# Weight loads of a two-part kernel on ScalarE's queue instead of SyncE's, and one preparation item a product later

## The chip, the cores and the metric

The kernel runs on one core of a Trainium2 chip. The metric is the time of one execution on the device in microseconds (us). Engines are called TensorE (PE in the profile; PEld is its weight load), VectorE (DVE), ScalarE (ACT), GpSimd (POOL) and SyncE (SP). A transfer (DMA) is issued by an engine in the order of that engine's instructions, goes into that engine's queue, and is carried out by 16 DMA engines that all queues share.

## The reference

The input `x` is 4 x 1024 x 1024 in float32. With `xn` the layer norm of `x`, the output is `x + s * g`:

```python
# s: an attention without softmax, over 4096 tokens of 1024 features
q, k, v = xn @ Wq.T + bq, xn @ Wk.T + bk, xn @ Wv.T + bv
kv = cumsum((elu(k) + 1) * v, axis=1)
s = ((elu(q) + 1) * kv * 64 ** -0.5) @ Wo.T + bo
# g: tokens are dispatched to 8 experts by the router's top 2, at most 256 places an expert;
# all experts have the same weights
h = gelu(buf @ w1.T + b1) @ w2.T + b2          # w1 4096 x 1024, w2 1024 x 4096
g = silu(sum over kept places of h * probability)
```

A token that no expert keeps has g = 0 there, and its output is `x`.

## The kernel before

Every product in float32 precision is made of three float32r matmuls: each operand is split into a high part (a cast by ScalarE, line 863) and a low part (VectorE's subtraction of the high part, line 866), and high x high, high x low and low x high are added up.

**The first part** (to about 453 us of the profiled execution) normalizes tokens, multiplies by Wk and Wv, makes the running sums, and routes the tokens. **The second part** has the 2048 chosen tokens, in two halves of 1024 (p = 0 and p = 1). For each half come five pairs of matrix products: four slices of the hidden layer (`hidden`, features x tokens, then `ffn_out`, tokens x outputs), and then `queries` with Wq and `result` with Wo. Each of these ten matrix products is done by a scheme of seven block products instead of eight, so there are 140 block products in a row, 14 for each pair, 48 matmuls each. They are called products 1 to 140 here; p = 1 begins with product 71.

The second part is written in steps, one for each product, step n beside product n. `on(n, phase, f)` puts a piece of work into a step, and the steps are emitted in an order by hand that every engine and SyncE's queue keep:

```python
PHASES = ("load", "pre", "cast0", "evac", "low0", "add", "cast1", "mid", "low1", "post", "raw")
for n in range(-4, n0 + 2):
    if 1 <= n <= n0:
        multiply(n)
    for phase in PHASES: ...        # the pieces of step n
```

What the next product needs is made in step n: the high parts of its two halves in `cast0` and `cast1`, the low parts in `low0` and `low1`. Each half has a buffer of its own out of three for a side (`Unit`), so a buffer is free when the product half that used it, three halves back, is done. `evac` adds up finished products, `add` and `post` make the sums of blocks that the scheme needs (line 1045, `sub`), and `raw`, the last phase, issues loads of weights.

There are two sorts of loads:

- **Raw weights** (tiles `raw`, five buffers of 128 x 4 x 512): quarters of a weight matrix, 1 MB a load, that ScalarE and VectorE turn into operands. `left_weights` (through `left_quarter`, line 834) loads those of w1 and Wq, `right_weights` (line 1184) those of w2. Four loads come in the four steps before the matrix product that uses them. A load waits until the tile's last reader is done.
- **Right operands that are stored ready** (tile `b`, line 1091, `fetched`): the tokens' operands (`xtd`, written on the way when the first slice of a half needs them, or by `xprep_items`) and those of Wo (`wod`, by `wprep_items`). They are loaded in phase `load` of the step before their product, in two halves of 1 MB.

Both sorts are issued by SyncE, in the order of the steps.

In the first half, three other pieces of work lie beside the products. `xprep_items` gathers the tokens of the second half and writes their operands, in steps 13 to 19 and 28 to 34; `wprep_items` does it for Wo, in four items of six stages that begin in steps 8, 20, 25 and 37 (load by GpSimd, then sums and subtractions of VectorE, casts of ScalarE, stores by GpSimd); and `queries` gathers the running sums. All their transfers go through GpSimd's queue (q0 in the profile). SyncE's queue is q1, ScalarE's q10.

Of the kernel before, what the change touches and what calls it, by code (L numbers as in the profile page):

```python
# [46 lines left out]
def tile_first_tokens(  # L47
# [17 lines left out]
    nc = tc.nc  # L65
# [107 lines left out]
    def split(dst, src):  # L173

        nc.scalar.copy(dst[0], src)  # L175
        nc.vector.tensor_tensor(dst[1], src, dst[0].bitcast(F32), ALU.subtract)  # L176
# [65 lines left out]
    def in_turn(ins):  # L242

        tc.keep_in_program_order(ins)
        return ins
# [477 lines left out]
    def wprep_items(w, buf):  # L723

        def item(a, k):
            v = {}

            def fetch():  # L730
                for j in range(2):
                    r = buf(f"wr_{a}_{k}_{j}")
                    for i in range(2):
                        v[i, j] = r[:, i * BT : (i + 1) * BT]
                        row = w[j, 2 * i + a].rearrange("p k f -> p (k f)")
                        in_turn(nc.gpsimd.dma_start(v[i, j], row[:, k * BT : (k + 1) * BT]))

            def out_of(i, src):
                o = buf(f"wo_{a}_{k}_{i}")
                oh = o.bitcast(F32R).rearrange("p (h t) -> h p t", h=2)  # L740
                split((oh[0], oh[1]), src)
                dst = wod.rearrange("(i p) (u h k t) -> i p u h k t", i=7, u=2, h=2, k=2)[i - 1]
                in_turn(
                    nc.gpsimd.dma_start(dst[:, a, :, k], o.rearrange("p (h t) -> p h t", h=2))  # L744
                )

            def sums():
                t = buf(f"wt_{a}_{k}")
                v["t1"], v["t2"] = t[:, :BT], t[:, BT:]
                nc.vector.tensor_tensor(v["t1"], v[0, 1], v[0, 0], ALU.subtract)  # L750
                nc.vector.tensor_tensor(v["t2"], v[1, 1], v["t1"], ALU.subtract)

            def out1():
                out_of(1, v[0, 0])
                out_of(2, v[1, 0])

            def out2():
                out_of(6, v["t2"])
                nc.vector.tensor_tensor(v[1, 0], v[1, 0], v["t2"], ALU.subtract)
                out_of(4, v[1, 0])  # L760

            def out3():
                out_of(3, v[1, 1])
                nc.vector.tensor_tensor(v[0, 1], v[1, 1], v[0, 1], ALU.subtract)
                out_of(7, v[0, 1])

            def out4():
                out_of(5, v["t1"])

            return fetch, sums, out1, out2, out3, out4  # L770

        return [item(a, k) for a in range(2) for k in range(2)]
# [56 lines left out]
        nc.vector.tensor_tensor(work[:, 2], work[:, 3], work[:, 2], ALU.subtract)  # L829
        nc.vector.tensor_tensor(ht, work[:, 2], work[:, 0], ALU.add)  # L830

    def left_quarter(dst, src, i, j):

        nc.sync.dma_start(
            dst.rearrange("p m (k f) -> p m k f", k=4),
            src[4 * i : 4 * i + 4, :, 4 * j : 4 * j + 4].rearrange("m p k f -> p m k f"),
        )
# [40 lines left out]
    raw = [early.tile([P, 4, BT], F32, name=f"raw_{i}") for i in range(2)]  # L878
# [138 lines left out]
    def on(n, phase, f):  # L1017
        hooks.setdefault((n, phase), []).append(f)
# [25 lines left out]
    def sub(dst, a, b):  # L1044
        nc.vector.tensor_tensor(dst, a, b, ALU.subtract)  # L1045

    def plus(dst, a, b):
        nc.vector.tensor_tensor(dst, a, b, ALU.add)  # L1048
# [17 lines left out]
    def built(n, side, src, halves, view):  # L1066

        units = plan_at(n)[side]
        plan_at(n)[side + "view"] = view
        if n == 1:  # L1070
            units.update(enumerate(begun[side]))
            return
        for u in range(2):

            def cast(u=u):
                x = Unit(side, 2 * n + u)
                x.cast(halves(src())[u])
                units[u] = x

            on(n - 1, f"cast{u}", cast)  # L1080
            on(n - 1, f"low{u}", lambda u=u: units[u].low())
# [66 lines left out]
    def left_weights(n0, src, order):  # L1148

        if order == ROWS:  # L1150
            tiles = ((0, 0), (1, 0), (1, 1), "t", (0, 1))
            loads = ((-4, (0, 0)), (-3, (1, 0)), (-2, (1, 1)), (-1, (0, 1)))
            if n0 % PASS == 0:

                loads = ((-10, (0, 0)), (-9, (1, 0)), (-8, (1, 1)), (-6, (0, 1)))
            on(n0, "add", lambda: sub(q["t"], q[0, 0], q[1, 0]))
            on(n0 + 1, "pre", lambda: plus(q[1, 0], q[1, 0], q[1, 1]))
            on(n0 + 1, "pre", lambda: sub(q[0, 0], q[1, 0], q[0, 0]))
        else:
            tiles = ((0, 0), (0, 1), (1, 0), (1, 1), "t")  # L1160
            loads = ((-4, (0, 0)), (-3, (0, 1)), (-2, (1, 0)), (-1, (1, 1)))
            on(n0 + 1, "add", lambda: sub(q["t"], q[0, 0], q[1, 0]))

            on(n0 + 1, "post", lambda: sub(q[0, 0], q[1, 1], q["t"]))
            on(n0 + 2, "add", lambda: plus(q[1, 0], q[1, 0], q[1, 1]))
        on(n0 + 3, "add", lambda: sub(q[0, 1], q[0, 1], q[0, 0]))
        q = dict(zip(tiles, raw))
        raw[:] = (q[k] for k in ((0, 0), "t", (1, 0), (1, 1), (0, 1)))
        for d, key in loads:

            if n0 or d > -3:
                on(max(n0 + d, -1), "raw", lambda key=key: left_quarter(q[key], src, *key))
        of = {1: (0, 0), 2: (0, 1), 3: (0, 1), 4: (1, 1), 5: (1, 0), 6: (0, 0), 7: "t"}
        for k, i in enumerate(order):
            built(n0 + 1 + k, "a", lambda i=i: q[of[i]], by_blocks, of_blocks)

    def right_weights(n0, src):

        q = dict(zip(((0, 0), (0, 1), (1, 1), "t", (1, 0)), raw))
        raw[:] = (q[k] for k in ("t", (0, 1), (0, 0), (1, 1), (1, 0)))  # L1180

        def load(key):
            i, j = key
            nc.sync.dma_start(
                q[i, j].rearrange("p (a k) f -> p a (k f)", a=2),
                src[j, 2 * i : 2 * i + 2].rearrange("a p k f -> p a (k f)"),
            )

        for d, key in ((-4, (0, 0)), (-3, (0, 1)), (-2, (1, 1)), (-1, (1, 0))):
            on(n0 + d, "raw", lambda key=key: load(key))  # L1190

        def t1():
            sub(q["t"], q[0, 1], q[0, 0])
            sub(q[0, 1], q[1, 1], q[0, 1])

        on(n0 - 1, "post", t1)
        on(n0, "post", lambda: sub(q[0, 0], q[1, 1], q["t"]))
        on(n0 + 5, "add", lambda: sub(q[1, 0], q[1, 0], q[0, 0]))
        for k, key in enumerate(((0, 0), (1, 0), (0, 0), "t", (0, 1), (1, 1), (1, 0))):
            built(n0 + 1 + k, "b", lambda key=key: q[key], by_chunks, all_chunks)  # L1200
# [38 lines left out]
    def features(n0, p, src, act, then=None, order=ROWS):  # L1239

        h = dict(hq)
        left_weights(n0, src, order)
        right_tokens(n0, p, order)
        if order == ROWS:
# [64 lines left out]
    def hidden(n0, p, s):  # L1309
        def act(dst, src, i, j):  # L1310
            for m in range(4):
                fc = s * DC + i * 4 + m
                nc.scalar.activation(dst[:, m], src[:, m], AF.Gelu, bias=b1[:, fc : fc + 1])  # L1313

        return features(
            n0, p, w1[s * DC : (s + 1) * DC], act, order=ROWS if s else FIRST
        )
# [206 lines left out]
    n0 = 0  # L1524
    for p in range(NP):
        y = dict(yq)
        if p == 0:
            for k, f in zip((8, 20, 25, 37), wprep_items(wo[0], small)):
                for d, stage in zip((0, 1, 1, 2, 3, 4), f):
                    on(n0 + k + d, "post" if d else "load", stage)  # L1530
        if p + 1 < NP:
            prep = xprep_items(p + 1, small)
            ats = ((0, 2, 2, 2, 2, 3, 3, 3, 4), (2, 4, 4, 5, 4, 5, 5, 6, 6))
            for j, (k, at) in enumerate((k, at) for k in (13, 28) for at in ats):
                for i, (d, f) in enumerate(zip(at, prep[j])):
                    on(n0 + k + d, "post" if i else "load", f)
        for s in range(NQ):
            h = hidden(n0, p, s)
            ffn_out(n0 + 7, h, s, y)
            n0 += 14  # L1540
        h = queries(n0, p)
        finals(n0, y, p)
        result(n0 + 7, h, y, p)
        n0 += 14
# [87 lines left out]
```

## Time and profile before

| | us |
|---|---|
| median of 3 runs | 2049.31 |
| lowest, highest | 2042.5, 2054.33 |
| the profiled execution's own time | 2028.41 |
| its span, first to last instruction | 2026.6 |
| products 1 to 140 | 453 to 2006 |

| transfers in the profile's list | issued by | count | KB each |
|---|---|---|---|
| b<-xtd, b<-wod | SyncE | 126, 28 | 1024 |
| raw<-in_w, raw<-in_wq | SyncE | 64, 8 | 1024 |
| xtd<-o, wod<-wo | GpSimd | 28, 28 | 512 |
| wr<-in_wo | GpSimd | 16 | 256 |
| kvs<-kr (first part) | ScalarE | 32 | 256 |

A line of a timeline gives the start in us, the duration (of merged instructions from the first start to the last end), engine, line of the program, operation and tiles, and in brackets the idle time before it and what ended that. A q behind an engine's name (SPq) marks its instruction sequencer: for a transfer it is the issue, not the transfer itself. Starts of products are taken from the trace: every 48th matmul of line 1121.

### The profile page before, as it was taken

Reading aid. Unit: us, or ns where it says so; the run is one execution under the profiler, and the core shown is the slowest. Engines: PE = TensorE matmul, PEld = TensorE weight load, DVE = VectorE, ACT = ScalarE, POOL = GpSimd, SP = SyncE. Lnnn points to the kernel's source line nnn. Section 1 sums busy time; section 2 is a strip of 40 time slices with the busy share of each in tenths; the row PEclk is TensorE's granted clock in tenths of the full one; section 3 lists DMA queues with packets and bytes.
Section 4 is the critical chain, followed back from the end, with each engine's and each line's share of the span. In section 5 each row is a group of like instructions: output and inputs, shape, how many; then the busy total and the mean of one; then the engine's idle time right before and its main releaser. Section 6 shows DMA issues by size and latency. Waiting matters only on the chain.

```text
span 2026.6 us, 22522 instructions
## 1 busy us (share of the span) xinstructions
PE 1973.7 (97%) x8872; PEld 1627.0 (80%) x8872; DVE 1509.2 (74%) x1422; ACT 747.8 (37%) x876; POOL 413.5 (20%) x403
## 2 busy tenths in 40 slices
PE   8999999999999999999899999999999999999995
PEld 7877878788888787887688888888888888888884
DVE  7868876488897896894497796596586586697794
ACT  3323332225534443542242452352342342342460
POOL 2001103550043124117203015500000000303014
PEclk9999999999999999999799999999999999999998
DMA  8768848638359559547515579814614614715567
GB/s 313 239 198 239 270 133 177 188 123 306 112 203 347 208 203 368 218 150 246 196 46 196 185 241 324 296 42 166 249 42 167 249 42 166 270 44 195 187 203 152
DMA packets 121011, 400.17 MB, mean 197 GB/s; under 512 B 13792, under 2 KB 38368, under 8 KB 99168
## 3 DMA queue, kind: packets, MB, share of 16 engines
q1 hardware_dynamic: 79360, 320.95, 45.7%
q0 software_dynamic: 23104, 61.43, 10.1%
q10 hardware_dynamic: 18432, 16.26, 3.5%
q8 instruction: 72, 1.18, 0.2%
q14 instruction: 43, 0.35, 0.0%
HBM read 317.83 MB, written 88.10 MB: 200 GB/s over the span
## 4 chain that ended last, share of the span: by engine, by line
PE 92%; DMA 3%; DVE 2%; issue 1%; ACT 0%; POOL 0%; SPq 0%; ACTq 0%; DVEq 0%; POOLq 0%
PE ps L1121 73%; PE pv L169 9%; PE pk L169 9%; DMA b<-xtd 2%; PE pl L339 1%; DMA wr_w<-in_wk 0%; DVE xt L176 0%; POOL out L1469 0%; DVE raw L1045 0%; PE pr L349 0%; DMA kvs<-kr 0%; ACT xt L175 0%; DVE ks L418 0%; DVE ws_w L176 0%; DVE pt L249 0%
## 5 line engine op out<-in xcount | busy, mean ns | idle before, releaser
L1121 PE MATMUL ps<-b,a 128*128 128x512 f32 x6720 | 1536.4, 391 | 16.4 <-issue 9.9
L1121 PEld LDWEIGHTS ps<-b,a 128*128 128x128 f32 x6720 | 1265.3, 188 | 287.3 <-issue 23.6
L866 DVE TENSOR_TENSOR a<-raw,a 128x1024 fp32r<-128x1024 f32 x140 | 170.5, 1220 | 203.9 <-ACT a L863 189.5
L863 ACT CAST a<-raw 128x1024 fp32r<-128x1024 f32 x140 | 147.1, 1052 | 457.1 <-PE ps L1121 344.7
L661 POOL DMA_INDIRECT gk<-kvs,eighth x128 | 146.8, 1147 | 614.4 <-DVE kv L249 576.1
L863 ACT CAST a<-hid 128x1024 fp32r<-128x1024 f32 x120 | 125.6, 1050 | 279.3 <-PE ps L1121 237.5
L169 PE MATMUL pk<-xt,ws_w 128*128 128x512 f32 (+1 forms) x792 | 185.2, 390 | 3.0 <-ACT xt L175 2.2
L169 PE MATMUL pv<-xt,ws_w 128*128 128x512 f32 (+1 forms) x792 | 180.8, 384 | 1.2 <-DVE ws_w L176 1.2
L866 DVE TENSOR_TENSOR a<-hid,a 128x1024 fp32r<-128x1024 f32 x120 | 146.0, 1218 | 41.7 <-ACT a L863 41.6
L169 PEld LDWEIGHTS pk<-xt,ws_w 128*128 128x128 f32 x792 | 147.4, 192 | 34.4 <-ACT xt L175 2.7
L169 PEld LDWEIGHTS pv<-xt,ws_w 128*128 128x128 f32 x792 | 144.7, 188 | 30.8 <-DVE ws_w L176 2.1
L1048 DVE TENSOR_TENSOR hid<-ps,hid 128x2048 f32<-128x2048 f32 (+1 forms) x69 | 125.1, 1820 | 51.7 <-PE ps L1121 36.2
L1045 DVE TENSOR_TENSOR raw<-raw,raw 128x2048 f32<-128x2048 f32 x62 | 141.8, 2287 | 0.8
L866 DVE TENSOR_TENSOR b<-raw,b 128x1024 fp32r<-128x1024 f32 x112 | 136.3, 1217 | 0.0
L863 ACT CAST b<-raw 128x1024 fp32r<-128x1024 f32 x112 | 117.3, 1047 | 0.0
L1048 DVE TENSOR_TENSOR work<-ps,work 128x2048 f32<-128x2048 f32 x40 | 91.4, 2285 | 30.2 <-PE ps L1121 30.2
L175 ACT CAST ws_w<-wr_w 128x1024 fp32r<-128x1024 f32 x64 | 66.0, 1048 | 82.2 <-issue 31.6
L176 DVE TENSOR_TENSOR ws_w<-wr_w,ws_w 128x1024 fp32r<-128x1024 f32 x64 | 77.7, 1214 | 13.0 <-ACT ws_w L175 9.6
L1313 ACT ACTIVATE hid<-hid,bs 128x512 f32<-128x512 f32 x104 | 66.7, 713 | 52.5 <-DVE hid L1048 52.5
L375 ACT ACTIVATE kb<-pk,bs 128x512 f32<-128x512 f32 (+1 forms) x40 | 25.8, 645 | 144.5 <-PE pk L169 100.8
L744 POOL DMA_DIRECT2D wod<-wo x28 | 20.2, 722 | 264.8 <-DVE wo L176 245.0
L214 POOL TENSOR_TENSOR r<-ve,mhalf 128x1 f32<-128x1 f32 x18 | 22.9, 1275 | 220.7 <-DVE ve L212 220.7
(183 smaller groups left out, 1293.6 us busy)
## 6 DMA issues: line engine op xcount, KB each, us to landing
b<-xtd SPq DMA_DIRECT2D x126, 1024.0 KB
raw<-in_w SPq DMA_DIRECT2D x64, 1024.0 KB
b<-wod SPq DMA_DIRECT2D x28, 1024.0 KB
wr_w<-in_wk SPq DMA_DIRECT2D x32, 512.0 KB
wr_w<-in_wv SPq DMA_DIRECT2D x32, 512.0 KB
xtd<-b SPq DMA_DIRECT2D x14, 1024.0 KB
wod<-wo POOLq DMA_DIRECT2D x28, 512.0 KB
xtd<-o POOLq DMA_DIRECT2D x28, 512.0 KB
```

The lines of the kernel that those rows point to most:

```text
L169: nc.tensor.matmul(ps, ws[:, w, k], mv[:, x, k, c0:c1], start=n == 0, stop=n == len(order) - 1)
L175: nc.scalar.copy(dst[0], src)
L176: nc.vector.tensor_tensor(dst[1], src, dst[0].bitcast(F32), ALU.subtract)
L214: nc.gpsimd.tensor_tensor(r, ve, mhalf, ALU.pow)
L375: nc.scalar.activation(kb, ps, AF.Identity, bias=bcol)
L661: nc.gpsimd.indirect_dma_start(out=dst, out_offset=None, in_=src, in_offset=bass.IndirectOffsetOnAxis(ap=idx, axis=0),)
L863: nc.scalar.copy(self.parts[0], src)
L866: nc.vector.tensor_tensor(self.parts[1], self.src, self.parts[0].bitcast(F32), ALU.subtract)
L1045: nc.vector.tensor_tensor(dst, a, b, ALU.subtract)
L1048: nc.vector.tensor_tensor(dst, a, b, ALU.add)
L1121: nc.tensor.matmul(ps[m] if s["apart"] else ps[:, m], a(h, k, m), b(l, k), start=s["first"] and u == 0 and k == 0 and i == 0, stop=u == 1 ...
L1313: nc.scalar.activation(dst[:, m], src[:, m], AF.Gelu, bias=b1[:, fc : fc + 1])
```

## The change

`left_quarter` is given a queue. Loads of raw weights by `left_weights` that fall into a step after step 0 are issued by ScalarE, and so are all those of `right_weights`; they stand at the same place in the steps, but now in the order of ScalarE's instructions. The two loads of the first part and the two of the prologue stay with SyncE, and the loads of stored operands stay there too. The second item of `wprep_items`, all six of its stages, begins in step 21 instead of 20.

```diff
-    def left_quarter(dst, src, i, j):
-
-        nc.sync.dma_start(
+    def left_quarter(dst, src, i, j, queue=nc.sync):
+
+        queue.dma_start(
             dst.rearrange("p m (k f) -> p m k f", k=4),
             src[4 * i : 4 * i + 4, :, 4 * j : 4 * j + 4].rearrange("m p k f -> p m k f"),
         )
...
             if n0 or d > -3:
-                on(max(n0 + d, -1), "raw", lambda key=key: left_quarter(q[key], src, *key))
+
+                queue = nc.scalar if n0 + d > 0 else nc.sync
+                on(
+                    max(n0 + d, -1), "raw",
+                    lambda key=key, queue=queue: left_quarter(q[key], src, *key, queue),
+                )
...
         def load(key):
             i, j = key
-            nc.sync.dma_start(
+            nc.scalar.dma_start(
                 q[i, j].rearrange("p (a k) f -> p a (k f)", a=2),
                 src[j, 2 * i : 2 * i + 2].rearrange("a p k f -> p a (k f)"),
             )
...
         if p == 0:
-            for k, f in zip((8, 20, 25, 37), wprep_items(wo[0], small)):
+            for k, f in zip((8, 21, 25, 37), wprep_items(wo[0], small)):
                 for d, stage in zip((0, 1, 1, 2, 3, 4), f):
                     on(n0 + k + d, "post" if d else "load", stage)
```

## The prediction

> **What bounds the kernel now.** I read the page first, then the chain of work that ended last, then the busy times by stretch, then the timelines of single engines around the places where TensorE lost time. The page:
>
> ```profile
> PE 1973.7 (97%) x8872; PEld 1627.0 (80%) x8872; DVE 1509.2 (74%) x1422; ACT 747.8 (37%) x876; POOL 413.5 (20%) x403
> q1 hardware_dynamic: 79360, 320.95, 45.7%
> q10 hardware_dynamic: 18432, 16.26, 3.5%
> ```
>
> TensorE (PE) is busy 97% of the span, so a change that adds no matmul can win only from the 3%. The queue that SyncE fills is q1, ScalarE's is q10. From the chain, four of its pieces:
>
> ```profile
> 453.42 195.88 PE ps L1121 x864
> 649.32 11.81 DMA b<-xtd
> 793.94 12.86 DMA b<-xtd
> 819.72 11.72 DMA b<-xtd
> ```
>
> The first piece gives the unit: 195.88 / 864 = 0.2267 us a matmul, 48 of them = 10.88 us a product. The others say that late right operands (tile b) end waits near products 19 to 21 and 32 to 35. The busy times by stretch, cut at starts of products, say how much that costs (columns: stretch, its length, busy us and count of PE, PEld, DVE, ACT, POOL, granted clock, DMA share, GB/s):
>
> ```profile
> 605.60:649.12 43.52, 43.52 (x193) 36.05 (x192) 31.67 (x31) 17.98 (x23) 18.33 (x18) 1.00 0.91 326
> 649.12:684.94 35.82, 33.13 (x145) 26.88 (x144) 29.07 (x25) 16.55 (x22) 6.44 (x9) 1.00 0.86 344
> 793.74:842.55 48.81, 45.65 (x193) 37.03 (x192) 36.43 (x34) 23.32 (x33) 11.55 (x15) 0.97 0.95 366
> 951.35:993.40 42.05, 31.64 (x98) 21.31 (x96) 10.60 (x10) 6.71 (x9) 19.59 (x20) 0.72 0.60 215
> 1211.00:1255.24 44.24, 44.05 (x194) 35.89 (x192) 29.71 (x18) 8.43 (x8) 19.11 (x11) 1.00 1.01 314
> 1418.44:1461.96 43.52, 43.52 (x194) 36.04 (x192) 21.44 (x14) 13.31 (x16) 0.00 (x0) 1.00 0.76 274
> ```
>
> Subtract 10.88 for each product. 649.12 holds three: 35.82 - 32.64 = 3.18 lost. 793.74 holds four: 48.81 - 43.52 = 5.29. 1211.00 holds four: 0.72. 951.35 holds two: 42.05 - 21.76 = 20.29, but there the clock is 0.72 and no line names an operand; I count nothing of it for the change. 605.60 and 1418.44 lose nothing. So the second part loses 9.2 us to late operands, all of it in the first 1024 slots, where GpSimd's queue carries the other half's tokens. In 1418.44 the same operand and weight loads run without GpSimd (POOL 0.00) and nothing is late.
>
> Why they are late, from SyncE's and TensorE's timelines:
>
> ```profile
> 649.32 5.76 SPq L1091 DMA_DIRECT2D b<-xtd  x2
> 655.13 0.48 SPq L1184 DMA_DIRECT2D raw<-in_w  x1
> 660.20 7.11 SPq L1091 DMA_DIRECT2D b<-xtd  x2
> 661.27 11.12 PE L1121 MATMUL ps<-b,a 128*128 128x512 f32 x48 [1.10 <-DMA b<-xtd]
> 806.94 23.63 PE L1121 MATMUL ps<-b,a 128*128 128x512 f32 x96 [2.15 <-DMA b<-xtd]
> ```
>
> A raw load of 1 MB stands in q1 between two operand loads. Counting the trace's packets from 644 to 678 us, q1 moved 253 KB/us and GpSimd's q0 153, together 406. An operand half issued at 660.20 waits for the raw load issued at 655.13 and is there only near 673.9, 13.7 us on; its own 1049 KB at 253 KB/us would be 4.1.
>
> **The change, part by part.** *The move.* The DMA list has 72 raw loads (64 of in_w, 8 of in_wq). Two are issued before the second part and two in its prologue; 68 go to q10. On SyncE only operand loads stay, and each is issued when its buffer comes free. Two operand halves a product are 2097 KB / 10.88 = 193 KB/us. If the three queues take turns by descriptor (from 655 to 668 us q0 and q1 did 586 and 568), b's 8 KB pieces against 4 KB of raw and 4 KB of q0 may have half of 406, 203: enough. I take all three losses as gone: -9.2; the other end, nothing gone, is a rival below.
>
> *Issue on ScalarE.* One load took SyncE 0.38 to 1.57 us (L1184), ScalarE's own stores (L438) 0.31 to 1.55. 68 x 0.41 = 28 us, at L438's median of 0.95 it is 65, spread at one a product over an engine that is busy 37%. Cost on the path 0, hidden by ScalarE's idle time. Without that cover each would push back a cast by its 0.4 to 0.95.
>
> *The wait on ScalarE.* A raw load waits until its tile was last read, by VectorE. On SyncE nothing but loads stood behind it; now the next product's casts do. I compared all 68 issue times with the start of the next cast: five come later than it, issue included, by 0.2 to 2.6 us. The worst are the loads of 721.35 and 730.90:
>
> ```profile
> 721.35 9.91 SPq L834 DMA_DIRECT2D raw<-in_w  x2
> 719.17 1.05 ACT L863 CAST a<-hid 128x1024 fp32r<-128x1024 f32 x1 [2.25 <-DVE hid L1045]
> 724.05 1.21 DVE L866 TENSOR_TENSOR a<-hid,a 128x1024 fp32r<-128x1024 f32 x1
> ```
>
> The cast of 719.17 moves to 721.75 and ends at 722.8; its consumer, VectorE's subtraction, starts only at 724.05, since VectorE is full there. The second: 731.3, ends 732.3, consumer 732.99. Cost 0, with 0.7 to 1.2 us to spare.
>
> *The raw loads come later and slower.* This is the price. In step 17 ScalarE reaches the load's place after the cast of another operand at 643.29, so at 643.9; SyncE issued it at 637.34. Three loads are then in q10, 3146 KB. What b leaves, 406 - 193 = 213, is shared with q0: 107 KB/us each, 29.4 us, so the third lands at 673.3. Its user is the second of VectorE's two subtractions at 669.27. With the waits gone the middle of product 20 is 1.35 earlier and that subtraction could start at 670.2: 3.1 late. The products from 21 on also come 1.75 earlier against VectorE than before (TensorE's wait at 673.98 had given it that). VectorE is thus 4.85 behind.
>
> *The item moved a product on* takes work out of just these steps: sums and two subtractions (2.74 us) leave step 21; by the end of steps 22 and 23 VectorE has done 2.05 less, by the end of 24 0.68 less. Its four loads and its stores on GpSimd go one product on with it; nothing else of GpSimd lies in step 21. What VectorE had in hand (its last subtraction for a product against that product's start) was 3.4 at product 23, 1.37 at 24, 0.73 at 25, 2.06 at 26. Late then: 23: 4.85 - 2.74 - 3.4 < 0; 24: 1.4; 25: 2.1; 26: 4.85 - 0.68 - 2.06 = 2.1. These are one delay, not a sum: +2.1. Around product 34 the same working (130 + 260 KB/us, 98 for raw, first issue near 798) gives 1.3 to 2.4 late plus 1.17, against 3.06 in hand: 0 to 0.5, I take 0.2.
>
> *Sum.* -9.2 + 2.1 + 0.2 = -6.9. Bounds: -9.2 if the raw loads are never late. Other end: if q0 keeps its present 153 (130) KB/us, raw gets 60 (67) and lands 26 and 16 us late: delays of 25 and 14, net +30. I take equal turns, because the 586 to 568 row shows them. The profiled execution took 2028.41 (span 2026.6 and 1.8 around it): 2021.5. The median of the runs shown is 20.9 above that execution; the difference is carried over: 2049.3 - 6.9 = 2042.
>
> *A rule against the change.* The row first: 366 GB/s and 0.95 of the DMA engines' time at 793.74. The Trainium skill, "DMA: Bandwidth & Descriptors", section "Issuing engines are not separate DMA queues", says that loads started by different engines interleave on the same 16 DMA engines, and that a second issuer only saves issue time; by it alone the sum would be 0 and the time 2049. The trace agrees on bandwidth, but 1418.44 loses nothing with the same loads, so I count order, not bandwidth, as what is late.
>
> **The rivals.** *More than the profile shows.* The timed runs are 14 to 26 us above the profiled one. The wait before 806.94 was followed by a product half of 7.15 instead of 5.44 at a clock of 0.97 on average; if half of the 20.9 is such waits and what follows them, another 10 goes: 2032. Against: the one large loss on record (951.35) shows no operand wait.
>
> *Slower: raw loads starve.* Same mechanism as my +2.1, at a lower rate for q10. At 75 KB/us the third loads are 15.6 and 11.1 us late, delays 14.6 and 9.2: 23.8 - 9.2 = +14.6, 2064. It decides below about 91 KB/us, where both delays make up 9.2. It ends at 2079. For it: VectorE has no idle time near product 25 (DVE 10.88 of 10.88), so nothing is caught up there. Against: the descriptors took turns.
>
> ```profile
> 717.58:728.46 10.88, 10.88 (x49) 9.01 (x48) 10.88 (x8) 4.01 (x4) 2.91 (x5) 1.00 0.54 180
> ```
>
> *Nothing.* The late halves are late on the DMA engines whatever the queue: 2049.
>
> **How the numbers follow.** A measurement of this kernel can tell about 0.5% from no change, 10.2 us: 2039.1 and 2059.6. My forecast 0.44; its 6.9 lies inside, but medians of runs that scatter by 6 put it on either side: same 0.26, faster 0.18. More than shown 0.22: faster. Starved 0.25: slower 0.22, same 0.03. Nothing 0.09: same 0.06, faster 0.02, slower 0.01. Together faster 0.42, same 0.35, slower 0.23. The range reaches from 2022 (the forecast with nearly all of the 20.9 gone) to 2068 (past the third case's 2064, short of its end); the forecast's own is 2036 to 2048.
>
> **What would show it.** q10 at 16.26 + 68 x 1.049 = 87.6 MB, q1 at 249.6. No PE wait named b<-xtd; the stretches of products 19 to 21 and 32 to 35 at 10.88 a product. VectorE waiting for raw before L1045 in products 20 and 34, by about 3 and 2 us, and TensorE waiting for VectorE near products 24 to 26. Wrong if b is still named, if those VectorE waits are over 8 us, or if ScalarE's casts wait behind loads by more than the subtraction after them.

## The result: slower by half a per cent

| | before | after |
|---|---|---|
| median of 22 runs of each on one chip (us) | 2048.52 | 2055.62 |
| lowest, highest | 2030.33, 2063.6 | 2041.29, 2062.99 |
| ratio, 95% interval | | 1.0049 [1.0031, 1.0068] |
| the profiled execution, its mean granted clock | 2028.41, 0.986 | 2041.29, 0.984 |

The forecast was 2042, faster by 6.9. The time stays inside the range and the ratio just inside the 0.5% that counted as no change, but the interval excludes 1 on the wrong side. Both profiled executions are among the quickest of their kernels, so the traces are compared with each other (+12.9 us), not with the medians. The one of before is quicker than all 22 runs of the table, and it is the only trace of that kernel.

In the page of after the queues are as the change meant them:

```profile
PE 1978.5 (97%) x8872; PEld 1627.0 (80%) x8872; DVE 1510.1 (74%) x1422; ACT 746.6 (37%) x876; POOL 416.2 (20%) x403
q1 hardware_dynamic: 51648, 249.64, 35.4%
q10 hardware_dynamic: 46144, 87.56, 13.2%
```

The queues carry 249.64 and 87.56 MB, as forecast; PE is busy 4.8 us longer with the same 8872 matmuls. From the chain of waits that ended last:

```profile
658.00 14.47 DMA raw<-in_w
...
1293.84 17.33 another core or an unknown queue
1311.18 6.20 DMA b<-xtd
```

There are no pieces of operands b near products 19 to 21 and 32 to 35 any more, a raw load comes into the chain in their place, and from 1293.84 on stand two pieces that before did not have. The busy times by stretch say what each place costs (columns as in the prediction; the last line is the kernel before at products 71 to 77):

```profile
649.31:681.95 32.64, 32.64 (x146) 27.03 (x145) 24.27 (x19) 15.42 (x20) 6.44 (x9) 1.00 0.93 373
714.59:737.35 22.76, 22.38 (x97) 17.86 (x96) 22.07 (x18) 10.34 (x13) 4.32 (x7) 1.00 0.60 207
802.63:836.87 34.24, 33.19 (x145) 26.87 (x144) 24.43 (x22) 13.13 (x19) 8.15 (x11) 1.00 1.01 394
836.87:860.39 23.52, 22.35 (x97) 17.86 (x96) 22.19 (x16) 13.89 (x17) 0.00 (x0) 1.00 0.07 26
936.55:998.05 61.50, 43.82 (x145) 30.33 (x144) 16.95 (x14) 8.62 (x10) 33.44 (x33) 0.78 0.51 179
1215.65:1259.17 43.52, 43.52 (x193) 36.04 (x192) 29.25 (x18) 8.44 (x8) 18.38 (x11) 1.00 1.01 316
1291.81:1323.09 31.28, 25.51 (x98) 18.95 (x97) 11.77 (x8) 6.55 (x8) 13.19 (x14) 0.89 0.61 227
```

```profile
1244.25:1320.52 76.27, 76.27 (x337) 63.14 (x337) 47.41 (x28) 26.69 (x30) 45.43 (x38) 1.00 0.86 290
```

With 10.88 a product taken off, and single products taken from their starts in the trace where stretches differ:

| products | lost before | forecast | lost after |
|---|---|---|---|
| 19 to 21 | 3.18 | 0 | 0 |
| 22 to 26 | 0 | 2.1 | 1.0 |
| 32 to 35 | 5.29 | 0 | 1.6 |
| 36 and 37 | 0 | 0.2 | 1.8 |
| 45 to 47 | 20.3 | not counted | 28.9 |
| 68 to 71 | 0.72 | 0 | 0 |
| 75 and 76 | 0 | 0 | 9.5 |

Where operands were late before, or sums were feared late, 9.2 became 4.4, and no wait for an operand is among the 4.4. One such wait is left in the second part, 1.07 us at 1317.52 in product 76, behind the slow stretch there. But 18.1 us were added at products 45 to 47 and 75, 76, where no operand and no changed transfer was expected to matter. TensorE's and GpSimd's timelines there:

```profile
969.05 0.59 PE L1121 MATMUL ps<-b,a 128*128 128x512 f32 x1 [0.83 <-issue]
971.15 1.52 PE L1121 MATMUL ps<-b,a 128*128 128x512 f32 x2 [1.51 <-issue]
...
981.74 0.59 PE L1121 MATMUL ps<-b,a 128*128 128x512 f32 x1 [1.52 <-issue]
983.13 12.14 PE L1121 MATMUL ps<-b,a 128*128 128x512 f32 x40 [0.80 <-issue]
```

```profile
959.87 0.95 POOL L661 DMA_INDIRECT gk<-kvs,eighth  x1 [0.31 <-issue]
...
962.37 0.94 POOL L661 DMA_INDIRECT gk<-kvs,eighth  x1 [0.30 <-issue]
```

TensorE issues one or two matmuls at a time with 0.8 to 1.5 us between them, and nothing in the profile holds it ("issue"). Beside it GpSimd issues the gathers of `queries` (tile gk, line 661), most of them 1.25 us apart. There are 48 in a row from 907.6 to 979.7; TensorE slows down from 943.6 on and issues without gaps again from 983.13. At 75 and 76 there are 32 in a row, 1264.6 to 1309.0, and it is the same:

```profile
1304.83 0.49 PE L1121 MATMUL ps<-b,a 128*128 128x512 f32 x1 [0.32 <-issue]
...
1307.63 1.01 PE L1121 MATMUL ps<-b,a 128*128 128x512 f32 x2 [0.92 <-issue]
1309.75 6.71 PE L1121 MATMUL ps<-b,a 128*128 128x512 f32 x20 [1.10 <-issue]
```

The 20.29 us that the prediction set aside in before look the same: gathers from 908.4 to 976.7, TensorE with gaps until 980.3. Before has the 32 gathers beside products 72 to 76 too (1260.2 to 1304.1), and there they cost it nothing.

### The profile page after: what moved, and what is told of

The parts are those of the page before. It is cut to its first block, busy times and chain, and to the rows that moved or that the text cites. A ratio compares the mean times of both kernels' runs of the same rounds, so it can differ in the third digit from the quotient of the medians.

```text
span 2039.5 us, 22467 instructions
## 1 busy us (share of the span) xinstructions
PE 1978.5 (97%) x8872; PEld 1627.0 (80%) x8872; DVE 1510.1 (74%) x1422; ACT 746.6 (37%) x876; POOL 416.2 (20%) x403
## 3 DMA queue, kind: packets, MB, share of 16 engines
q1 hardware_dynamic: 51648, 249.64, 35.4%
q10 hardware_dynamic: 46144, 87.56, 13.2%
## 4 chain that ended last, share of the span: by engine, by line
PE 83%; DVE 7%; issue 3%; DMA 3%; ACT 1%; another core or an unknown queue 1%; POOL 1%; SPq 0%; ACTq 0%; DVEq 0%; POOLq 0%
PE ps L1121 65%; PE pv L169 8%; PE pk L169 8%; DVE a L866 1%; DVE b L866 1%; PE pl L339 1%; DVE hid L1048 1%; DMA xtd<-o 1%; DMA raw<-in_w 1%; DVE work L1048 1%; DVE raw L1045 0%; DVE wo L176 0%; POOL g L661 0%; DMA b<-xtd 0%
## 5 line engine op out<-in xcount | busy, mean ns | idle before, releaser
L176 DVE TENSOR_TENSOR ws_w<-wr_w,ws_w 128x1024 fp32r<-128x1024 f32 x64 | 77.8, 1215 | 13.0 <-ACT ws_w L175 10.2
```

## The experiments

The runs met several chips. On some the kernel before shows a mean clock of 0.98 to 0.99 and medians of 2035 to 2049 us ("chips at 0.98": the first one was of that sort), on others 0.994 and 1996 to 1997 us. Times are compared only with the kernel before on the same chip. Losses of single products are taken from starts in the trace, as above.

**Is the loss one of a part of the change, or of the gathers?** First the parts, on one chip at 0.994. The queue alone (`e1_queue_only`, in the changed kernel):

```diff
-            for k, f in zip((8, 21, 25, 37), wprep_items(wo[0], small)):
+            for k, f in zip((8, 20, 25, 37), wprep_items(wo[0], small)):
```

> The changed kernel with the second item back in step 20: the queue alone. Theory A: the change is slower because raw loads go through ScalarE's queue while GpSimd issues its long unbroken runs of gathers (48 in products 42 to 46, 32 in products 72 to 76), where TensorE is slow in both kernels; the item has no part in it. Then this is near 2056, as the changed kernel, with 0 to 3 us more lost at products 22 to 26. Theory B: the item moved into step 25 is what costs. Then this is at or below 2049. Theory C: the slower time is scatter of the runs: 2044 to 2052.

Measured: 1998.68 against 1996.77, 1.0010 [0.9996, 1.0023]. Products 22 to 25 lose 6.3. Here the third raw load is later than in after:

```profile
667.90 2.29 DVE L1045 TENSOR_TENSOR raw<-raw,raw 128x2048 f32<-128x2048 f32 x1 [5.62 <-DMA raw<-in_w]
```

VectorE waits 5.62 us, and with the item's first sums still in step 21 (line 750 at 679.05) it does not catch up. With the item moved, traces in which the load came 5.0 to 5.9 late lost 3.9 to 4.8 at products 22 to 26 (below). So the moved item seems to relieve these steps by some 2 us. No wait for an operand is left in this trace either: it is the queue that took them away. The item alone (`e2_item_only`) keeps all loads on SyncE and only makes the 20 a 21.

> The kernel before with the second item alone moved from step 20 to 21; all raw loads in SyncE's queue. Theory A: the item only makes room behind late raw loads, which do not come late here: no difference from the kernel before (-2 to +2 us). Theory B: VectorE is full in products 24 to 27, so the item moved into step 25 costs by itself: 2 to 6 us, lost at products 24 to 27.

Measured: 1998.49 against 1997.02, 1.0011 [0.9999, 1.0023]. Late operands still cost 4.5 (products 19, 20, 34). The whole change on that chip (`a_after`, and once more `after_again`; no edit):

> The changed kernel itself once more, beside the kernel before. Where the granted clock of the kernel before is near 0.98 (as in the first comparison): 2050 to 2060 against 2044 to 2052, with products 45 to 47 slow. Where it is near 0.994 (as in the last four runs): no slow products 45 to 47 and a difference of -4 to +3 us, since only the operand waits and VectorE's late sums count there.

> The changed kernel beside the next three. Where the clock of the kernel before is near 0.98: 5 to 10 us above the kernel before, with slow stretches at products 45 to 47 or 75 to 76. Where it is near 0.994: -4 to +1, no slow stretch.

Measured: 0.9989 [0.9975, 1.0003] and 0.9999 [0.9985, 1.0013]. From product 2 on the second part loses 4.6 and 6.4, and nothing of the slow stretches is there:

```profile
903.00:965.00 62.00, 61.95 (x273) 50.99 (x273) 34.14 (x27) 16.28 (x17) 49.50 (x42) 1.00 0.85 307
```

That is the stretch of the same 48 gathers in `a_after`: TensorE busy 61.95 of 62.00, clock 1.00. So on a chip at 0.994 TensorE is not slowed beside the gathers, and the change is worth nothing that can be measured; the forecast of 0.9966 lies outside both intervals. The profiled executions agree: after's span is 46.6 us longer than `a_after`'s (2039.5 against 1992.9); the losses of the second part differ by 34.8 (42.9 against 8.1, of which 3.4 in product 1), and 12.0 is the later start of the second part (453.4 against 441.4). The 12.0 have nothing to do with the change, for before starts it at 453.3. But they seem to be of the same kind: in the first part GpSimd issues 18 and then 32 other indirect transfers (tiles lst and gx, from 321.3 and 370.7 in after), and beside them all seven traces at 0.98 show gaps of TensorE that nothing in the profile ends, 5.7 to 9.6 us of them together, and none of the 13 traces at 0.994 shows one.

**Do loads in ScalarE's queue beside the gathers matter?** `e3_not_in_bursts` gives the loads of the steps beside gathers back to SyncE, `e4_only_in_bursts` is the reverse, the kernel before with only those moved to ScalarE. The edit of the first:

```diff
+BURSTS = (*range(42, 50), *range(72, 77))
...
-                queue = nc.scalar if n0 + d > 0 else nc.sync
+                queue = nc.scalar if n0 + d > 0 and n0 + d not in BURSTS else nc.sync
...
+                n0 + d, "raw",
+                lambda key=key, queue=nc.sync if n0 + d in BURSTS else nc.scalar: load(key, queue),
```

> The changed kernel, but the raw loads of steps 42 to 49 and 72 to 76 are issued by SyncE as before. Theory A: keeps the 4.8 us that operands no longer wait (products 19 to 21, 32 to 37, 68 to 71) and gives back what products 45 to 47 and 75 to 76 lost more than before (18 us in the two profiles): 2040 to 2046, products 75 and 76 at 10.88. Theory B or a queue that costs wherever it is used: stays at 2053 to 2058.

> The kernel before with only the raw loads of steps 42 to 49 and 72 to 76 in ScalarE's queue, and no other edit. Where the clock of the kernel before is near 0.98, theory A (loads of ScalarE's queue during the long runs of gathers make TensorE's slow stretch longer): 8 to 18 us slower than the kernel before. Rival (the slow stretch has nothing to do with the queue): -3 to +3. Where the clock is near 0.994 and no slow stretch is there, both: -3 to +3.

Measured: 1.0010 [0.9998, 1.0022] and 1.0005 [0.9990, 1.0019], both on a chip at 0.994, which has no slow stretches: they can't tell of them. `e4_only_in_bursts` lost 7.7 to late operands, as the kernel before would.

**Spreading the gathers.** In `p_before` and `p_after` four gathers go into each step, held to it by a small instruction of VectorE that GpSimd waits for; in `pl_before` and `pl_after` only the start of each of the four fetches is held:

```diff
         def fetch(i, j):
+            in_turn(nc.gpsimd.tensor_scalar(seen, pace, 1.0, None, ALU.add))
...
+        def tick():
+            nc.vector.tensor_scalar(pace, bq1[:, 0:1], 1.0, None, ALU.add)
...
+            on(n0 + k - 1, "post", tick)
```

> The kernel before with the gathers of queries paced: four gathers a step in 16 steps instead of 16 at once, each four held back by a tiny VectorE instruction of the step before; nothing is left out. If TensorE's slow stretch at products 45 to 47 comes from gathers without a pause, those 20 us go and the granted clock there is 1.00: 2022 to 2034. If it comes from anything else (TensorE's own load, the stage of the program), it stays: 2045 to 2052.

> The changed kernel with the same pacing. Theory A: without long runs of gathers the queue can cost nothing, and what is left is the 4.8 us of operand waits: 3 to 7 below the paced kernel before, 2016 to 2030. Theory B and a queue that costs everywhere: still 5 to 10 above the paced kernel before.

> The kernel before with the same four holds. Near clock 0.98, if long runs of gathers make the slow stretch: 15 to 25 us below the kernel before; if not, within 3. Near clock 0.994: within 3 of the kernel before.

> The changed kernel with each of the four fetches of queries (16 gathers) held back until the step it is written for, by one tiny VectorE instruction: no run of gathers is longer than 16, where there were 48 and 32. Near clock 0.98, if long runs of gathers make TensorE's slow stretch: 20 to 35 us below the changed kernel, and the same as the paced kernel before less 2 to 5. If not: within 3 of the changed kernel. Near clock 0.994: within 3 of the changed kernel under both.

Measured, all at 0.994: 1.0018 [1.0004, 1.0033], 1.0010 [0.9997, 1.0023], 1.0017 [1.0002, 1.0032], 1.0006 [0.9993, 1.0018]. Where there are no slow stretches, spreading the gathers costs the kernel before 3 to 4 us; for the changed kernel the intervals include 1. `n_before` and `n_after` leave out the gathers, and with them the choice of rows (their expectation says what stands in their place):

```diff
-            for jj in range(4):
-                slots[2 * p + j].eighths(
-                    g[jj // 2][:, jj % 2 * BT : (jj % 2 + 1) * BT], kvs, i, jj
-                )
+            for half in range(2):
+                in_turn(nc.gpsimd.dma_start(g[half], kvs[half * P : (half + 1) * P, :]))
```

> The kernel before without the gathers of queries: each fetch of 16 gathers is replaced by two plain transfers of 512 KB from fixed rows (left out: the choice of rows). Where the clock of the kernel before is near 0.98: if the gathers make TensorE's slow stretches, 20 to 30 us below the kernel before and no slow product 45 to 47; if not, within 3. Where it is near 0.994, where the traces show no slow stretch: within 3 of the kernel before.

> The changed kernel without the same gathers. Theory (the queue gains 3 to 5 us of operand waits, loses 1 to 4 of them to late sums, and was slower in the first comparison only through the slow stretches beside gathers): 0 to 4 below the same kernel before without gathers, on either chip. Rival (the queue costs wherever it is used): on a chip with clock near 0.98 it stays 5 to 10 above.

Measured: 0.9988 [0.9974, 1.0002] and 0.9989 [0.9973, 1.0005], again on a chip at 0.994. Without gathers both kernels are alike: `n_before` loses 8.0, mostly to late operands, `n_after` 6.8, mostly to late sums. The saved waits are given back, almost in full, without these gathers too.

**Is it ScalarE's place in the order?** `e5_late` puts the preparation stages into a phase of their own behind the raw loads, so that ScalarE reaches the loads earlier:

```diff
-        "load", "pre", "cast0", "evac", "low0", "add", "cast1", "mid", "low1", "post", "raw"
+        "load", "pre", "cast0", "evac", "low0", "add", "cast1", "mid", "low1", "post", "raw", "late"
...
-                    on(n0 + k + d, "post" if d else "load", stage)
+                    on(n0 + k + d, "late" if d else "load", stage)
```

> The changed kernel with the stages of the token and Wo preparation in a phase of their own behind the raw loads, so that in steps 17 to 20 and 31 to 34 ScalarE issues a raw load before the casts of those stages. Theory (the third raw load is late because ScalarE comes late to it): VectorE no longer waits for raw before its sums in products 20 and 34, and the 1.0 us at products 25 and 26 and the 2 us at 36 and 37 shrink to under 1 together: 2 to 3 below the changed kernel. Rival (it is late because three queues share the DMA engines): no less than now is lost there, 0 to 3 above.

Measured: 1.0014 [0.9999, 1.0028]. VectorE waits for no raw load in this trace, and products 22 to 26 lose 0.5, where the other traces of the changed kernel on these chips lose 1.0 to 6.3: so ScalarE's place in the order is part of what makes the load late. But the stages that now come later cost more than that gains. Product 18 loses 2.2 and product 33 alone 6.1; there TensorE waits 5.96 us for ScalarE's cast of the token preparation.

**Back on a chip at 0.98**, where the kernel before took 2041.38. The changed kernel (`after_fourth`), the same with the first of each four loads of w2 on SyncE again (`e7_first_sync`), that with the loads beside gathers on SyncE too (`e8_first_sync_no_bursts`), and `e7_first_sync` with the fetches held as in `pl_after` (`pl_e7`):

```diff
-            nc.scalar.dma_start(
+            queue.dma_start(
...
+                lambda key=key, queue=nc.sync if d == -4 else nc.scalar: load(key, queue),
```

> The changed kernel, to be compared with the three below on the same chip. Clock of the kernel before near 0.994: -3 to +1 us against it. Near 0.98: +5 to +10.

> The changed kernel with the first of each four loads of right_weights (four steps ahead) issued by SyncE, the other three by ScalarE. Theory: only two loads share the DMA engines with the operands when the second and third are wanted, so VectorE's sums in products 20 and 34 are not late and products 22 to 26, 36 and 37 lose under 1.5 us together instead of 3 to 5; operands stay on time: 2 to 4 below the changed kernel. Rival (the sums are late through ScalarE's place and VectorE's own work, not the queue's length): within 1 of the changed kernel, the same products lose as much.

> As the kernel above, and the raw loads of steps 42 to 49 and 72 to 76 by SyncE too. Clock near 0.994: within 1.5 of the kernel above. Near 0.98, if loads in ScalarE's queue lengthen the slow stretches beside gathers: 5 to 15 below the kernel above; if not: within 3.

> As the first-by-SyncE kernel, with the four fetches of queries held to their steps, so that no run of gathers is longer than 16. Clock near 0.994: 0 to 2 above that kernel. Near 0.98, if long runs of gathers make the slow stretches: 20 to 35 below it; if not, within 3.

| | ratio, 95% interval | lost at 45 to 47 | at 75 and 76 | at the early products |
|---|---|---|---|---|
| `after_fourth` | 1.0029 [0.9999, 1.0059] | 31.9 | 10.3 | 6.6 |
| `e7_first_sync` | 1.0028 [1.0002, 1.0054] | 27.2 | 10.2 | 3.4 |
| `e8_first_sync_no_bursts` | 1.0016 [0.9990, 1.0041] | 29.0 | 9.8 | 1.8 |
| `pl_e7` | 0.9874 [0.9841, 0.9907] | 12.8 | 0 | 3.3 |

In `e7_first_sync` products 22 to 26, 36 and 37 lose 1.7 in place of the 5.9 of `after_fourth`, but 1.7 come back at product 32, 1.5 of them a wait for an operand, and the medians lie only 0.2 us apart.

Three things follow. The slow stretches are as long with no changed load beside them (`e8_first_sync_no_bursts`) as with all of them: the loads in ScalarE's queue during the gathers are not what lengthens them. The medians say so too (2046.49 and 2046.99). At the early products `e8_first_sync_no_bursts` loses only 1.8, where before lost 9.2, and its time still shows no gain: by these traces the stretches cover it. And holding four fetches takes 27 us off (2046.78 to 2019.72), the clearest sign that the gathers make the stretches. In `pl_e7` the run of 48 gathers has become 32 and 16; products 45 and 46 still lose 12.8 beside the 32. The hold also takes the gathers of the second half away from products 72 to 76: 32 of them in a row now lie at products 111 to 116 and cost 0.3. So a run's length isn't all that counts.

Last, `pg_e7`: `pl_e7` with the second fetch a step later, so that no run is longer than 16.

```diff
-            (-14, 2, (0, 0)), (-12, 2, (1, 1)), (-6, 3, (1, 0)), (1, 3, (0, 1))
+            (-14, 2, (0, 0)), (-11, 2, (1, 1)), (-6, 3, (1, 0)), (1, 3, (0, 1))
```

> Kernel pl_e7 with the second of the four fetches begun one step later, so that no run of gathers is longer than 16 (in pl_e7 one of 32 was left, 908.3 to 958.9, and products 45 and 46 still lost 4.34 and 8.42 us there). If a long unbroken run of gathers is what makes TensorE slow: on a chip where the kernel before shows a clock near 0.98, products 45 to 47 lose less than 3 us together, and the ratio to the kernel before is 0.980 to 0.985, below pl_e7's 0.9874. If the place in the sequence counts, and not the length of the run, products 45 to 47 still lose 8 to 13 us and the ratio stays at 0.987. On a chip where the kernel before shows 0.994 both give 1.000 to 1.002.

Measured on another chip: 2009.92 against 2034.82 (2013.59 to 2050.04), 0.9898 [0.9859, 0.9937], clock of the profiled execution 0.992. TensorE's timeline over the products that lost 28.9 in after is now one line (line 1122 is line 1121 of after):

```profile
904.69 95.68 PE L1122 MATMUL ps<-b,a 128*128 128x512 f32 x420
```

Nothing is lost at 45 to 47, as the theory of the run's length had it. Its six runs lie within 2.8 us (2007.98 to 2010.81), where those of the kernel before spread over 36.5 (25.7 without the slowest): the scatter seems to belong to the stretches. The ratio is not the 0.980 to 0.985 that was expected; on this chip the kernel before was 6.6 us quicker than on the last one, so there was less to win. Both `pl_e7` and `pg_e7` beat the kernel before on their chips, and `pl_e7` the changed one too (2046.99 beside it). Neither was run at 0.994, where the holds cost `pl_before` 3 us and `pl_after` nothing clear.

## Why the prediction was wrong

*The step that failed* is one sentence: of 20.29 us in products 46 and 47 "I count nothing of it for the change". It took the largest loss of the second part as a constant because no operand was named beside it. It isn't constant: it is made by something that the change doesn't touch, GpSimd's gathers, and it has a size of its own in each execution. The two profiles have 20.3 and 38.4 us of it; the runs of after go from 2041.29 at a mean clock of 0.984 to 2062.99 at 0.979, so much of their scatter goes with this clock. On the chip of `after_fourth` the runs of the kernel before and of the changed one follow nearly the same line, some 2.4 us for each 0.001 of clock (a fit to 29 and 12 runs). Their median clocks are 0.984 and 0.9815, which by that line is 6 us, and their medians differ by 5.6. So the time that the change adds there goes with the lower clock, as that of the slow stretches does. The 18.1 us of the pair of profiles are not the change's price: the medians differ by 7.1, and with the 1 to 5 us saved elsewhere (below) some 8 to 12 are left for the stretches, an estimate.

The rows shown already held a part of the hint: GpSimd busy 19.59 of 42.05 us in exactly that stretch. The busy column alone would not have told, for 605.60 has 18.33 of 43.52 and loses nothing; what GpSimd does there, gathers without a pause, only its timeline shows.

*The operand waits* went as forecast in products 19 to 21, 32 and 68 to 71, and in `e1_queue_only` as well, so order in the queue was what was late there. Part of the lateness only changed places: a raw load is now late at product 20's sums in every trace of the changed kernel and its variants but `e5_late`, by 1.1 to 5.9 us. The rule of the Trainium skill that the prediction weighed ("DMA: Bandwidth & Descriptors", section "Issuing engines are not separate DMA queues") gave 0 and 2049 for the time. On the time at 0.994 that was right, but not for its reason: in after 373 and 394 GB/s flow with the operands on time, and the gain was lost elsewhere.

*The raw loads' price.* The second subtraction was forecast to wait 3.1 for a load at 673.3; it waited 2.17, until 672.57. The equal share of 107 KB/us a queue came near: from 643.9 to 672.5 the packets of q10 carry 112 KB/us, those of q0 115 and those of q1 179. TensorE's loss from it was 1.0 at products 25 and 26, in place of 2.1. It varies: in `after_again`, `n_after`, `after_fourth` and `p_after` the load came 5.0 to 5.9 late, and products 22 to 26 lost 3.9 to 4.8. So the forecast lies between the executions, and that it does is luck as much as working.

*Products 33 to 37* are the mis-sized term of the sum: +0.2 forecast, 3.4 measured. VectorE did not wait for raw there at all (one such wait is in the trace, that of product 20); the forecast of 2 us was wrong. TensorE waits 0.67 for ScalarE (put down to its cast of o, the preparation of tokens) and 0.38 for VectorE at products 33 and 34. ScalarE had itself stood 7.93 us, until 807.32, for a store of that preparation in GpSimd's queue (xtd<-o; the longest such wait in before was 4.1), which the prediction's working has nowhere. At product 36 TensorE waits for VectorE's own run of work:

```profile
829.20 4.61 DVE L1045 TENSOR_TENSOR raw<-raw,raw 128x2048 f32<-128x2048 f32 x2
833.73 2.28 DVE L1048 TENSOR_TENSOR hid<-ps,hid 128x2048 f32<-128x2048 f32 x1
835.93 1.22 DVE L866 TENSOR_TENSOR a<-hid,a 128x1024 fp32r<-128x1024 f32 x1
837.06 1.22 DVE L866 TENSOR_TENSOR b<-raw,b 128x1024 fp32r<-128x1024 f32 x1
```

```profile
838.33 24.04 PE L1121 MATMUL ps<-b,a 128*128 128x512 f32 x103 [1.07 <-DVE b L866]
```

VectorE is without a gap from 829.20 on. In before TensorE lost 5.3 us in products 32 to 35, now 1.6; so the 3.06 that VectorE "had in hand" seem to have been partly the waits that were removed. No run tests this by itself. Outside the slow stretches the sum was thus -9.2 + 1.0 + 3.4 = -4.8 in this pair of traces, for -6.9, and about -1 with `n_before` and `n_after` (one trace each).

*ScalarE's issue* took 0.37 to 0.42 us a load, as forecast, and no wait of TensorE is put down to it. One load, at 810.72, stands just ahead of the casts before the 0.67 us wait, so a few tenths on the path are not excluded.

*The rivals.* "Raw loads starve" gave 2064 and is refuted: it needed loads 15.6 and 11.1 us late, no trace of the changed kernel has VectorE waiting more than 5.9 us for one load, and the slowness lies elsewhere. "More than the profile shows" gave 2032, and no run of after is below 2041.29. "Nothing" is nearest by a hair (0 against +14.6 for a measured +7.1), without being the reason.

*What stays open.* At 0.994 the change measured 0.9989 and 0.9999, at 0.98 1.0049 and 1.0029. That the difference lies in the slow stretches is shown for the profiled executions, and the clocks of the runs speak for it. What in the change makes them longer is not shown, and with one trace of the kernel before it is not known how long its stretches mostly are. By what means the gathers slow TensorE no run shows either. In the changed kernel the 48 gathers begin 3.6 us after the start of product 42, in before 0.5, and the 32 begin half a microsecond later in product 72 (with the item alone moved 3.2, with the loads of the steps beside gathers alone 1.2). That such a shift is enough to lengthen the stretches is only argued; all kernels run at 0.98 with the raw loads on ScalarE have it, and the item alone, which brings most of it, was not run at 0.98. Since `e8_first_sync_no_bursts` and the kernel before overlap (1.0016 [0.9990, 1.0041]), a small cost of the loads elsewhere isn't excluded either.

## What to carry to other kernels

When a trace shows a large loss that no wait explains, find what runs beside it before setting it aside as a constant: read the busy column and the timeline of every engine in that stretch, and look whether the loss ends when that work ends. Compare it in a second trace of the same kernel. Slack read from a schedule that waits is partly made of the waits; take it again after removing them. And a change worth a few microseconds is to be judged on more than one chip, because a loss of 20 to 40 us that some chips don't have can decide its sign.

## What the runs showed of the hardware

- On some chips an unbroken run of the gathers of `queries`, most of them 1.25 us apart, slows TensorE 36 to 48 us after it began: it issues one or two matmuls per 1.4 to 2.1 us with no wait on record, until about the end of the run. 48 in a row cost 20 to 32 us, 32 in a row 0 to 13 us, 16 in a row nothing in any trace. Other indirect transfers did it sooner: in the first part of before TensorE's gaps begin 18 and 21 us after the first of 18 and of 32. On chips at 0.994 the same 48 bring no such stretch; the largest loss in the products beside them was 0.8 us, in product 48.
- In such a stretch the granted clock was 0.5 for 23.9 us (965.1 to 989.0 in after). The Trainium skill, "TensorE: Matmul & The Clock Gate", section "Part 1: The HAM clock gate", has half the clock after at least one idle window of about 3.4 us. Here the longest gap from 946 to 983 was 1.56 us; in the 3.4 us before the clock fell (to 948.0 and to 965.1) TensorE was busy 1.66 and 1.80 us. So many short gaps were enough here.
- Two chips of the same kind ran the same kernel before in 2048.5 and 1996.8 us (medians of 22 and 35 runs).
